# First sequence's projections by halves of the heads, and the last two ends in turn: attention with a routed feed-forward layer on one core

## The chip, the cores and the metric

One Trainium2 chip, of which the kernel uses one core. The metric is device time in microseconds (us) of one execution. PE is the matrix engine (PEld its weight loads), DVE the vector engine, ACT the scalar engine, POOL the GpSimd engine, SP the engine that here does nothing but issue DMAs (SPq and ACTq are the DMA queues that SP and ACT issue to).

## The reference

A batch x of 8 sequences of 1024 tokens, 256 wide, goes through one layer, all in float32.

```python
# attention, on layernorm(x); 16 heads of 16
q, kv = x @ Wq, x @ Wkv                       # keys and values are the same projection
q, kv = rotary(q) * SCALE, rotary(kv)
attn = softmax(einsum('bmd,bnd->bmn', q, kv)) # 1024 x 1024 per head
x = x + (einsum('bij,bjd->bid', attn, kv) @ Wout + bout)
# feed-forward, on layernorm(x), 8192 tokens, 8 experts
scores = softmax(xf @ gate_w.T)               # 8192 x 8
vals, idx = top_k(scores.T, 1024)             # each expert takes its 1024 best tokens
y = layernorm(xf[idx]) * ln_w + ln_b
out = (gelu(y @ fc1.T + b1) @ fc2.T + b2) * vals
x = x + xf.at[idx].add(out)
```

## The kernel before, in words

**Attention.** The 8 sequences (b) go one after the other. Each has four groups (g) of four heads; c = 0 and c = 1 are the two halves of the 256 columns, so the first two groups need c = 0 alone and the other two c = 1. A sequence has two halves hf of 512 tokens and T = 8 tiles t of 128 tokens. A group is 16 *steps*. Scores are needed twice: `row_max` (L425) makes four of the group's 64×128·512 products a step, and DVE takes each one's maximum over 512 keys (L440); 13 steps later (LEAD) `score_pass` (L479) makes the scores of one key tile for exp on ACT (L517), the maxima having been put in through `lay_max` (L444): maxima are transposed, copied to `mrows` (L468), written to DRAM as `top_d` (L470) and read back as rows `top` (L474). Every second step `weigh_values` (L527) multiplies exps and values. So the loop starts with 13 steps of maxima alone (s = −13 to −1), then runs maxima of one step and exps of another as *pairs*, and ends with exps alone.

**Prologue** (`prologue`, L316): for one sequence, x is normalised (statistics L185, scaled L208), transposed (L217) into `xnT`, multiplied with Wq and Wkv (L357, `ps_p`), and rotated (`rotate`, L220). Rotating takes two products with the sines (`u`, L236), one with the cosines (`pe`, L238), the sum `qk` (L239) and a copy into the value tiles `v_bufs` (L242). For b = 0 the products are on DVE and read PSUM; for later sequences ACT first copies to SBUF (L230) and all is on POOL. Then, for each c, hf and s (s = 0 queries, 1 keys), `qk` is transposed and `split_halves` (L261) makes two float32r parts `hi` and `lo`, which SP writes to DRAM (`q_d`, `k_d`, L257) twice over; `split_steps` (L289) does so with differences of neighbouring key tiles (`s_d`). `load_keys`, `load_steps` and `load_queries` (L396 to L420) read them back group by group.

**Epilogue** (`epilogue`, L602): for half a sequence, the attention output `ao` is transposed into `aoT` (L612), multiplied with Wout (L619, `ps_o`), added to the residual `xr` (L627), normalised to `xf` (L208), transposed (L661), multiplied with the gate (L667, `ps_g`), copied (`lg`, L675), transposed back (`ps_gt`, L678), put through a softmax over 8 experts (L681 to L693), transposed again (`ps_sc`), copied (`turned`, L700) and written into `by_expert` (L703); twice normalised rows go to `rows_d` in DRAM (L708).

**What sets the order.** The program is issued by hand in one order; every engine takes its instructions in that order. Prologues and epilogues are generators that stop at each `yield`. After each step `run_pieces` (L720) advances them: a piece of kind "x" is *heavy* and takes the one place that a step has while only maxima run and that every odd step has later; an integer is a wait of so many steps. `run_loads` (L758) issues loads when they are due and their data is written. Before the loop, the first prologue is advanced until the keys of c = 0 are written. After the loop `finish` runs the last sequence's two ends, first the half hf = 0, then hf = 1:

```python
        finish(urgent)
        for hf in range(2):
            if finished.pop((NG * B - 1, hf), None):
                ends.append(Task(epilogue(B - 1, hf)))
        finish(ends)
```

Tiles of a pool with one buffer per tag make the next user of the tag wait for the last: `aoT` serves `aoT` and `xfT`, `xf` the normalised rows, `lg` both `lg` and `turned`, `m` (four PSUM buffers) all of transposes, projections, maxima and weighted values.

**Selection and experts.** The 1024th best score of each expert is found by 30 rounds of bisection over `by_expert` (count L897, total over partitions L901, L904, L907); then places and token lists are made, rows gathered from `rows_d` (L1030), and the experts run (L1046 to L1084).

Of the kernel before, what the change touches and what calls it, by code (L numbers as in the profile page):

```python
# [19 lines left out]
P = 128  # L20
# [7 lines left out]
def preln_attention_moe_kernel(  # L28
# [58 lines left out]
        pattern=[[NB, E], [0, NB]], channel_multiplier=-1,  # L87
    )
    cand = [const.tile([P, 1], I32, name=f"cand{i}") for i in range(2)]

# [5 lines left out]
    with ExitStack() as actx:  # L96
# [120 lines left out]
                nc.tensor.transpose(pt[:, t * P : (t + 1) * P], src(t), ident)  # L217
            return pt

        def rotate(b, t, pp, qk):  # L220

            hd = DH // 2
            first = b == 0
            eng = nc.vector if first else nc.gpsimd
            if first:
                pe = side.tile([P, 2 * D], F32, tag="pe", name="pe")
                raw = pp
            else:
                pe = side.tile([P, 2 * D], F32, tag="pe", name="pe")
                nc.scalar.copy(pe, pp)  # L230
                raw = pe
            v4 = raw.rearrange("p (h a d) -> p h a d", a=2, d=hd)
            u = side.tile([P, 2 * H, DH], F32, tag="u", name="u")
            for a in range(2):
                s3 = sin[:, t, a, :].unsqueeze(1).to_broadcast([P, 2 * H, hd])
                eng.tensor_tensor(u[:, :, a * hd : (a + 1) * hd], v4[:, :, 1 - a, :], s3, ALU.mult)  # L236
            c4 = cos[:, t, :].unsqueeze(1).unsqueeze(1).to_broadcast([P, 2 * H, 2, hd])
            eng.tensor_tensor(pe.rearrange("p (h a d) -> p h a d", a=2, d=hd), v4, c4, ALU.mult)  # L238
            nc.gpsimd.tensor_tensor(  # L239
                qk.rearrange("p a d -> p (a d)"), pe, u.rearrange("p h d -> p (h d)"), ALU.add  # L240
            )
            kd = v_bufs[b % 2][:, t, 0 : H * VS].rearrange("p (h d) -> p h d", d=VS)[:, :, 0:DH]  # L242
            nc.gpsimd.tensor_copy(kd, qk[:, 1, :].rearrange("p (h d) -> p h d", d=DH))


        pending = []
# [14 lines left out]
        def split_halves(b, hf, c, s, pt):  # L261

            q_d, k_d, _ = halves[b]
            first = b == 0 and c == 0
            hi = side.tile([P, QW], F32R, tag="hi", name="hi")
            lo = side.tile([P, QW], F32R, tag="lo", name="lo")
            full = None
            if first:
                nc.scalar.copy(hi, pt)
                nc.vector.tensor_tensor(lo, pt, hi.bitcast(F32), ALU.subtract)  # L270
            if not first or s == 1:
                full = side.tile([P, QW], F32, tag="full", name="full")
# [12 lines left out]
            return full  # L285
# [30 lines left out]
        def prologue(b):  # L316

            q_d = dram.tile([2, D, 4, QW], F32, tag="q_d", name=f"q_d{b}", bufs=2)
            k_d = dram.tile([D, 4, N], F32, tag="k_d", name=f"k_d{b}", bufs=2)
            s_d = dram.tile([D, 4, N], F32, tag="s_d", name=f"s_d{b}", bufs=2)  # L320
            halves[b] = (q_d, k_d, s_d)
            if b == 0:
                xts = [xt_first, load_x(b, 1)]
            else:
                xts = [load_x(b, hf) for hf in range(2)]
                yield 6 if b == 1 else 2
            qks = []

            def normalised(hf):
                stats = yield from row_stats(xts[hf], "a", 2 if b == 0 else 1)  # L330
                scaled(nc.vector if b == 0 else nc.gpsimd, xts[hf], xts[hf], stats)

            yield from normalised(0)
            if b > 0:
                yield from normalised(1)
            yield 3
            for hf in range(2):
                yield "x"
                xnT = one.tile([P, DC, QW], F32, tag="T", name=f"xnT_{b}_{hf}")
                for c in range(DC):  # L340
                    pt = transposed(lambda t: xts[hf][:, t, c * P : (c + 1) * P])
                    nc.scalar.copy(xnT[:, c, :], pt)
                qk = side.tile([P, T2, 2, D], F32, tag="qk", name=f"qk_{b}_{hf}")
                qks.append(qk)
                if hf == 0:

                    yield (2 * T * NG * (b - 1) - 5,)
                other = normalised(1) if b == 0 and hf == 0 else None
                for j in range(T2):
                    if other is not None:  # L350
                        kind = next(other, None)
                        if kind is not None:
                            yield kind
                    yield "x"
                    pp = ps_m.tile([P, QW], F32, tag="m", name="ps_p")
                    for c in range(DC):
                        nc.tensor.matmul(  # L357
                            pp,
                            lhsT=xnT[:, c, j * P : (j + 1) * P],
                            rhs=wqkv[:, c].rearrange("p a d -> p (a d)"),  # L360
                            start=(c == 0),
                            stop=(c == DC - 1),
                        )
                    rotate(b, T2 * hf + j, pp, qk[:, j])
                if other is not None:
                    yield from other
            for c in range(DC):
                fulls = []
                for hf in range(2):
# [232 lines left out]
        def epilogue(b, hf):  # L602
# [3 lines left out]
            eng = nc.vector if last else nc.gpsimd  # L606
            xt = residual(b, hf)
            yield "x"
            aoT = one.tile([P, DC, QW], F32, tag="aoT", name=f"aoT_{b}_{hf}")
            for c in range(DC):  # L610
                pt = transposed(lambda t: ao[:, T2 * hf + t, c * P : (c + 1) * P])
                nc.scalar.copy(aoT[:, c, :], pt)  # L612
# [14 lines left out]
                nc.vector.tensor_tensor(sl, po, sl, ALU.add)  # L627

            stats = yield from row_stats(xt, "b")
            xf = one.tile([P, T2, D], F32, tag="xf", name=f"xf_{b}_{hf}")  # L630
# [27 lines left out]
            xfT = one.tile([P, DC, QW], F32, tag="aoT", name=f"xfT_{b}_{hf}")  # L658
# [168 lines left out]
        for hf in range(2):  # L827
            if finished.pop((NG * B - 1, hf), None):
                ends.append(Task(epilogue(B - 1, hf)))
        finish(ends)  # L830


    ctx.enter_context(tc.manual_schedule())
# [55 lines left out]
    with tc.tile_pool(name="ps_sel", bufs=2, space=PSUM) as ps_sel:  # L889
# [3 lines left out]
        now, then = cand  # L893
        nc.vector.memset(now, 1 << 29)
        for bit in range(29, -1, -1):
            cnt = it.tile([P, 1], F16, tag="cnt", name="cnt")
            nc.vector.tensor_scalar(  # L897
                ge, by_expert, now.bitcast(F32), None, ALU.is_ge, ALU.add, accum_out=cnt
            )
            tot = ps_sel.tile([P, 1], F32, tag="tot", name="tot")  # L900
            nc.tensor.matmul(tot, lhsT=same, rhs=cnt, start=True, stop=True)  # L901

            drop = it.tile([P, 1], I32, tag="drop", name="drop")
            nc.vector.tensor_scalar(  # L904
                drop, tot, float(K) - 0.5, float(1 << bit), ALU.is_lt, ALU.mult
            )
            nc.vector.scalar_tensor_tensor(  # L907
                then, drop, (1 << bit) >> 1, now, ALU.bitwise_xor, ALU.bitwise_xor
            )
            now, then = then, now  # L910
# [261 lines left out]
```

## Time and profile before

| | |
|---|---|
| runs | 2281.76, 2284.6, 2285.13 us; median 2284.6 |
| profiled execution, own time | 2283.41 us |
| its span in the trace | 2281.6 us |
| granted TensorE clock, mean | 0.962 |
| busy: PE, DVE, ACT, POOL | 2090.1 (92%), 1658.9 (73%), 1361.4 (60%), 1228.0 (54%) us |
| start, no maxima | 0 to 54.6 us |
| maxima alone | 54.6 to 94 us |
| maxima and exps in pairs | 94 to about 1660 us |
| exps alone | to about 1690 us |
| last two ends | to 1729.3 us |
| selection | to about 1790 us |
| experts | to 2281 us |

The stages are read from the timeline: the first maximum (L433) begins at 54.60, the first reduce after the first exps at 94.06, the first count (L897) at 1729.30. A matmul's end is modelled, so a busy PE may also be a slow or a waiting one. The granted clock is a share of full speed; the mean hides a stretch of 0.50 between 38 and 95 us. The execution's own time is 1.8 us more than its span.

### The profile page before, as it was taken

The page shows a single profiled execution, that of the slowest core. Times are in us where ns is not written, and L with a number is a line of the kernel's source. Part 1 is how long each engine was busy: PE and PEld are TensorE (multiplying, and loading weights), DVE is VectorE, ACT ScalarE, POOL GpSimd, SP SyncE. Part 2 cuts the span into 40 slices and gives each one's busy share as a digit, 9 for nine tenths or more (in the row PEclk, how much of TensorE's full clock was granted, in tenths as well). Part 3 has the DMA queues.
Part 4 walks back from the last instruction along what each step waited for, and adds up shares of the span by engine and source line. Part 5 has one row for each costly group of instructions (what it writes and reads, how often), then busy time and mean ns, then how long its engine had stood idle before and what let it go on. Part 6 is the DMA issues. An engine that isn't in the chain of part 4 may idle for free. (4 is left out here: it accounts for less than half of the span.)

```text
span 2281.6 us, 34611 instructions
## 1 busy us (share of the span) xinstructions
PE 2090.1 (92%) x12484; PEld 1106.4 (48%) x12484; DVE 1658.9 (73%) x3218; ACT 1361.4 (60%) x1742; POOL 1228.0 (54%) x1243
## 2 busy tenths in 40 slices
PE   4899899999999999999999999999971599999998
PEld 2444444444444444444444444444431366666665
DVE  4888888988898899889889988899926533333311
ACT  1378777877787877878777777778750011111111
POOL 4257658657584857758594765724331133333432
PEclk8699999999999999999999999999985699999999
DMA  4611633542363246236324722642113033332321
GB/s 162 244 66 67 242 113 132 204 166 88 122 236 101 85 173 238 81 121 233 118 76 171 248 76 87 219 153 86 45 43 112 20 75 75 75 72 66 78 38 27
DMA packets 154586, 275.67 MB, mean 121 GB/s; under 512 B 15152, under 2 KB 67760, under 8 KB 154288
## 3 DMA queue, kind: packets, MB, share of 16 engines
q1 hardware_dynamic: 140944, 254.80, 32.4%
q0 software_dynamic: 12288, 17.05, 4.6%
q8 instruction: 98, 1.61, 0.3%
q10 hardware_dynamic: 1184, 1.62, 0.2%
q14 instruction: 72, 0.59, 0.1%
HBM read 146.02 MB, written 127.14 MB: 120 GB/s over the span
## 5 line engine op out<-in xcount | busy, mean ns | idle before, releaser
L440 DVE TENSOR_REDUCE mx<-ps_x 128x1 f32<-128x512 f32 x2048 | 1265.1, 681 | 175.4 <-PE ps_x L433 161.5
L517 ACT ACTIVATE e<-ps_s 128x1024 f32<-128x1024 f32 x1024 | 995.8, 1025 | 102.2 <-PE ps_x L433 41.2
L433 PE MATMUL ps_x<-k,q 64*128 64x512 f32 x2048 | 727.2, 455 | 36.7 <-DMA q<-q_d 22.8
L484 PE MATMUL ps_s<-q,s 64*128 64x512 f32 x2048 | 621.8, 428 | 9.1 <-ACT e L517 5.8
L433 PEld LDWEIGHTS ps_x<-k,q 64*128 64x128 f32 x2048 | 352.0, 187 | 434.3 <-DVE mx L440 290.0
L536 PE MATMUL ps_av<-e,v 128*32 128x512 f32 x4096 | 494.0, 600 | 7.9 <-DVE mx L440 1.6
L551 POOL TENSOR_TENSOR av<-av,avp 128x512 f32<-128x512 f32 x191 | 243.3, 1274 | 411.6 <-ACT avp L549 400.7
L1066 ACT ACTIVATE hT<-ps_h,b 128x512 f32<-128x512 f32 x128 | 87.9, 687 | 431.3 <-PE ps_h L1059 431.3
L484 PEld LDWEIGHTS ps_s<-q,s 64*128 64x128 f32 x2048 | 313.7, 185 | 48.0 <-ACT e L517 30.4
L1084 POOL DMA_INDIRECT out<-o,idx x64 | 110.0, 1719 | 288.6 <-DVE o L1083 127.8
L1059 PE MATMUL ps_h<-yT,w 128*128 128x512 f32 x512 | 234.0, 604 | 0.9 <-DVE yT L1046 0.9
L1082 DVE TENSOR_TENSOR o<-ps_o,b2b 128x256 f32<-128x256 f32 x64 | 27.1, 424 | 282.2 <-PE ps_o L1074 282.2
L1074 PE MATMUL ps_o<-w,hT 128*128 128x256 f32 x1024 | 226.7, 380 | 0.0
L536 PEld LDWEIGHTS ps_av<-e,v 128*32 128x32 f32 x4096 | 107.3, 109 | 243.4 <-issue 163.8
L1074 PEld LDWEIGHTS ps_o<-w,hT 128*128 128x128 f32 x1024 | 192.8, 190 | 29.1 <-issue 4.3
L549 ACT COPY avp<-ps_av 128x512 f32<-128x512 f32 x192 | 112.6, 586 | 146.7 <-PE ps_av L536 144.1
L1059 PEld LDWEIGHTS ps_h<-yT,w 128*128 128x128 f32 x512 | 95.4, 192 | 102.0 <-issue 99.4
L357 PE MATMUL ps_p<-wqkv,xnT 128*128 128x512 f32 x256 | 127.5, 625 | 4.5 <-DVE mx L440 4.1
L1030 POOL DMA_INDIRECT g<-rows_d,idx x64 | 69.1, 1080 | 79.0 <-DVE idx L1023 59.8
L236 POOL TENSOR_TENSOR u<-pe,sin 128x256 f32<-128x256 f32 x112 | 79.2, 730 | 51.9 <-ACT pe L230 51.9
L275 POOL CAST hi<-full 128x512 fp32r<-128x512 f32 x60 | 36.7, 612 | 104.0 <-ACT full L273 73.9
L239 POOL TENSOR_TENSOR qk<-pe,u 128x512 f32<-128x512 f32 x64 | 81.7, 1277 | 15.6 <-DVE pe L238 11.2
(152 smaller groups left out, 1874.5 us busy)
## 6 DMA issues: line engine op xcount, KB each, us to landing
k<-k_d SPq DMA_DIRECT2D x64, 512.0 KB
q<-q_d SPq DMA_DIRECT2D x128, 256.0 KB
s<-s_d SPq DMA_DIRECT2D x64, 512.0 KB
q_d<-hi SPq DMA_DIRECT2D x32, 512.0 KB
q_d<-lo SPq DMA_DIRECT2D x32, 512.0 KB
k_d<-hi SPq DMA_DIRECT2D x32, 512.0 KB
k_d<-lo SPq DMA_DIRECT2D x32, 512.0 KB
s_d<-dhi SPq DMA_DIRECT2D x32, 512.0 KB
```

The source lines that it names most:

```text
L357: nc.tensor.matmul(pp, lhsT=xnT[:, c, j * P : (j + 1) * P], rhs=wqkv[:, c].rearrange("p a d -> p (a d)"), start=(c == 0), stop=(c == DC - 1),)
L433: nc.tensor.matmul(pt, lhsT=q[r : r + 64, h // 2, j * P : (j + 1) * P], rhs=k[r : r + 64, h // 2, kh * QW : (kh + 1) * QW], start=True, st ...
L440: nc.vector.tensor_reduce(grp[i]["mx"][:, kh, h, j : j + 1], pt, AX.X, ALU.max)
L484: nc.tensor.matmul(pt[:, h % 2, :], lhsT=ones_r[r : r + 64, :] if last else k[r : r + 64, pair, kt * P : (kt + 1) * P], rhs=(top_bufs[half ...
L517: nc.scalar.activation(e.rearrange("p h q -> p (h q)"), pt.rearrange("p h q -> p (h q)"), AF.Exp, scale=DH**-0.5,)
L536: nc.tensor.matmul(pa[HS * h : HS * (h + 1), :], lhsT=v_bufs[b % 2][:, kt, c : c + HS], rhs=es[h // 2][:, h % 2, :], start=(n == 0), stop= ...
L549: nc.scalar.copy(part, pa)
L551: (nc.vector if end else nc.gpsimd).tensor_tensor(av, av, part, ALU.add)
L1059: nc.tensor.matmul(ph, lhsT=weights[e][0][:, c, f * P : (f + 1) * P], rhs=yT[:, c, :], start=(c == 0), stop=(c == DC - 1),)
L1066: nc.scalar.activation(hT[:, f, :], ph, AF.Gelu_apprx_tanh, bias=b1[:, e * FC + f : e * FC + f + 1])
L1074: nc.tensor.matmul(po, lhsT=hT[:, f, j * P : (j + 1) * P], rhs=weights[e][1][:, f, :], start=(f == 0), stop=(f == FC - 1),)
L1084: nc.gpsimd.indirect_dma_start(out=out_rows[:, :], out_offset=bass.IndirectOffsetOnAxis(ap=idx[:, t : t + 1], axis=0), in_=o, in_offset=No ...
```

## The change

There are three edits.

1. *Prologue of the first sequence.* `project` and `rotate` take a column half c and a number n of halves. For b = 0 the projections of c = 0 alone (256 columns: q and k of 8 heads) are made for all eight tiles ahead of the loop; those of c = 1 are eight heavy pieces, each with its rotation, given out one to a step while the maxima run alone, and rotated by ACT and POOL as in later sequences. The second half's normalisation stands ahead of all projections, no longer between them. The second `xnT` of b = 0 takes the tag `aoT`, and the first two pairs of halves of the keys take a tile of the exps' tag `e`.
2. *Last two ends.* They are advanced in turn, one piece each. The second end (hf = 1) uses the tags `T` and `xr` where it used `aoT` and `xf`.
3. *Bisection.* The count (two tiles) and `drop` become fixed tiles, no longer tiles of the pool `it`.

```diff
+    counts = [const.tile([P, 1], F16, name=f"count{i}") for i in range(2)]
+    drop = const.tile([P, 1], I32, name="drop")
...
-        def rotate(b, t, pp, qk):
+        def rotate(b, t, pp, qk, c, n):
...
-            first = b == 0
+            first = b == 0 and c == 0
             eng = nc.vector if first else nc.gpsimd
+            W, nh = 2 * n * P, 2 * n * P // DH
+            pe = side.tile([P, 2 * D], F32, tag="pe", name="pe")[:, 0:W]
+            raw = pp
+            if not first:
                 nc.scalar.copy(pe, pp)
                 raw = pe
...
+        def project(b, t, xnT, qk, c, n):
+            pp = ps_m.tile([P, QW], F32, tag="m", name="ps_p")[:, 0 : 2 * n * P]
+            for kc in range(DC):
+                w = wqkv[:, kc, :, c * P : (c + n) * P]
+                nc.tensor.matmul(
+                    pp,
+                    lhsT=xnT[:, kc, t % T2 * P : (t % T2 + 1) * P],
+                    rhs=w.rearrange("p a d -> p (a d)") if n == DC else w,
+                    start=(kc == 0),
+                    stop=(kc == DC - 1),
+                )
+            rotate(b, t, pp, qk, c, n)
...
-            hi = side.tile([P, QW], F32R, tag="hi", name="hi")
-            lo = side.tile([P, QW], F32R, tag="lo", name="lo")
+            if first and s == 1:
+                both = prob.tile([P, 2, QW], F32R, tag="e", name="kl")
+                hi, lo = both[:, 0, :], both[:, 1, :]
+            else:
+                hi = side.tile([P, QW], F32R, tag="hi", name="hi")
+                lo = side.tile([P, QW], F32R, tag="lo", name="lo")
...
+            if b == 0:
+                xnTs = []
+                yield from normalised(0)
+                yield "x"
+                xnTs.append(turned(0))
+                yield from normalised(1)
+                for hf in range(2):
+                    if hf == 1:
+                        yield "x"
+                        xnTs.append(turned(1))
+                    for j in range(T2):
+                        yield "x"
+                        project(b, T2 * hf + j, xnTs[hf], qks[hf][:, j], 0, 1)
...
             for c in range(DC):
                 fulls = []
+                if b == 0 and c > 0:
+                    for t in range(T):
+                        yield "x"
+                        project(b, t, xnTs[t // T2], qks[t // T2][:, t % T2], c, 1)
...
-            aoT = one.tile([P, DC, QW], F32, tag="aoT", name=f"aoT_{b}_{hf}")
+            own = last and hf == 1
+            aoT = one.tile([P, DC, QW], F32, tag="T" if own else "aoT", name=f"aoT_{b}_{hf}")
...
-        finish(ends)
+        while ends:
+            for task in list(ends):
+                task.advance(n_steps)
+                if task.kind is None:
+                    ends.remove(task)
...
-            cnt = it.tile([P, 1], F16, tag="cnt", name="cnt")
+            cnt = counts[bit % 2]
...
-            drop = it.tile([P, 1], I32, tag="drop", name="drop")
```

More of the change, by code (lines that the diff above doesn't have):

```diff
@@ L218, in transposed @@
             return pt
-        def rotate(b, t, pp, qk):
+        def rotate(b, t, pp, qk, c, n):
             hd = DH // 2
-            first = b == 0
+            first = b == 0 and c == 0
             eng = nc.vector if first else nc.gpsimd
[L225 to L229, printed above, removed]
+            W, nh = 2 * n * P, 2 * n * P // DH
+            pe = side.tile([P, 2 * D], F32, tag="pe", name="pe")[:, 0:W]
+            raw = pp
+            if not first:
                 nc.scalar.copy(pe, pp)
@@ L232, in rotate @@
             v4 = raw.rearrange("p (h a d) -> p h a d", a=2, d=hd)
-            u = side.tile([P, 2 * H, DH], F32, tag="u", name="u")
+            u = side.tile([P, 2 * H, DH], F32, tag="u", name="u")[:, 0:nh, :]
             for a in range(2):
-                s3 = sin[:, t, a, :].unsqueeze(1).to_broadcast([P, 2 * H, hd])
+                s3 = sin[:, t, a, :].unsqueeze(1).to_broadcast([P, nh, hd])
                 eng.tensor_tensor(u[:, :, a * hd : (a + 1) * hd], v4[:, :, 1 - a, :], s3, ALU.mult)
-            c4 = cos[:, t, :].unsqueeze(1).unsqueeze(1).to_broadcast([P, 2 * H, 2, hd])
+            c4 = cos[:, t, :].unsqueeze(1).unsqueeze(1).to_broadcast([P, nh, 2, hd])
             eng.tensor_tensor(pe.rearrange("p (h a d) -> p h a d", a=2, d=hd), v4, c4, ALU.mult)
+            qk = qk[:, :, c * P : (c + n) * P]
             nc.gpsimd.tensor_tensor(
-                qk.rearrange("p a d -> p (a d)"), pe, u.rearrange("p h d -> p (h d)"), ALU.add
-            )
-            kd = v_bufs[b % 2][:, t, 0 : H * VS].rearrange("p (h d) -> p h d", d=VS)[:, :, 0:DH]
+                qk,
+                pe.rearrange("p (a d) -> p a d", a=2),
+                u.rearrange("p h d -> p (h d)").rearrange("p (a d) -> p a d", a=2),
+                ALU.add,
+            )
+            c0, c1 = c * P // DH * VS, (c + n) * P // DH * VS
+            kd = v_bufs[b % 2][:, t, c0:c1].rearrange("p (h d) -> p h d", d=VS)[:, :, 0:DH]
             nc.gpsimd.tensor_copy(kd, qk[:, 1, :].rearrange("p (h d) -> p h d", d=DH))
+        def project(b, t, xnT, qk, c, n):
[10 more added lines that the diff above has]
+            rotate(b, t, pp, qk, c, n)
         pending = []
@@ L331, in normalised, with turned @@
                 scaled(nc.vector if b == 0 else nc.gpsimd, xts[hf], xts[hf], stats)
[L333 to L339, printed above, removed]
+            def turned(hf):
+                tag = "aoT" if b == 0 and hf == 1 else "T"
+                xnT = one.tile([P, DC, QW], F32, tag=tag, name=f"xnT_{b}_{hf}")
                 for c in range(DC):
@@ L342, in prologue @@
                     nc.scalar.copy(xnT[:, c, :], pt)
[L343 to L353, printed above, removed]
-                    yield "x"
[L355 to L364, printed above, removed]
@@ L365, in prologue @@
-                if other is not None:
-                    yield from other
+                qks.append(side.tile([P, T2, 2, D], F32, tag="qk", name=f"qk_{b}_{hf}"))
+                return xnT
+            if b == 0:
[11 more added lines that the diff above has]
+                        project(b, T2 * hf + j, xnTs[hf], qks[hf][:, j], 0, 1)
+            else:
+                yield from normalised(0)
+                yield from normalised(1)
+                yield 3
+                for hf in range(2):
+                    yield "x"
+                    xnT = turned(hf)
+                    if hf == 0:
+                        yield (2 * T * NG * (b - 1) - 5,)
+                    for j in range(T2):
+                        yield "x"
+                        project(b, T2 * hf + j, xnT, qks[hf][:, j], 0, DC)
@@ L367, in prologue @@
             for c in range(DC):
                 fulls = []
+                if b == 0 and c > 0:
+                    for t in range(T):
+                        yield "x"
+                        project(b, t, xnTs[t // T2], qks[t // T2][:, t % T2], c, 1)
                 for hf in range(2):
@@ L629, in epilogue @@
             stats = yield from row_stats(xt, "b")
-            xf = one.tile([P, T2, D], F32, tag="xf", name=f"xf_{b}_{hf}")
+            xf = one.tile([P, T2, D], F32, tag="xr" if own else "xf", name=f"xf_{b}_{hf}")
             scaled(eng, xf, xt, stats)
@@ L657, in epilogue @@
             yield "x"
-            xfT = one.tile([P, DC, QW], F32, tag="aoT", name=f"xfT_{b}_{hf}")
+            xfT = one.tile([P, DC, QW], F32, tag="T" if own else "aoT", name=f"xfT_{b}_{hf}")
             for c in range(DC):
```

## The prediction

> **What bounds the kernel now.** I read the page first: PE 92% busy, DVE 73%, and its chain holds only the closing DMA, so it decides nothing here. The slices show where PE is not the bound: the first two and those around 1660 to 1790. The edits lie in just these places, so I read three timelines: start to first maximum, first maximum to first exp, last two ends to first count. A row gives start, duration, engine, line, operation, and in brackets the idle time before it with its releaser.
>
> The start:
>
> ```profile
> 10.23 1.38 DVE L208 TENSOR_SCALAR x<-x,mv_a,rs_a 128x256 f32<-128x256 f32 x4 [1.50 <-POOL rs_a L190]
> ...
> 34.18 0.37 SPq L257 DMA_DIRECT2D q_d<-hi  x1
> 34.63 1.26 POOL L239 TENSOR_TENSOR qk<-pe,u 128x512 f32<-128x512 f32 x1
> ...
> 54.60 6.52 PE L433 MATMUL ps_x<-k,q 64*128 64x512 f32 x12 [17.89 <-DMA q<-q_d]
> ```
>
> The first maximum waits for keys and queries that went through DRAM; their first write is issued at 34.18, just as POOL's last rotation sum begins. Between them the DMA engines are the limit. The windows (columns: stretch, length, busy time of PE, PEld, DVE, ACT, POOL, then granted clock, DMA share, GB/s) show them full to the end of the eight writes:
>
> ```profile
> 45.00:46.00 1.00, 0.00 (x0) 0.00 (x0) 0.00 (x0) 0.00 (x0) 1.00 (x3) 0.50 1.04 391
> 46.00:47.00 1.00, 0.00 (x0) 0.00 (x0) 0.00 (x0) 0.00 (x0) 0.94 (x2) 0.50 0.11 39
> ```
>
> So those 20.4 us (34.18 to 54.60) are bytes: they move as a block, and faster halves inside it gain nothing.
>
> The maxima, 54.6 to 94. DVE sets the pace (one maximum per 0.612 us, 2.45 a step of four) at a granted clock of 0.50, until a hole of over 4 us on PE and DVE:
>
> ```profile
> 81.25 0.51 SPq L257 DMA_DIRECT2D s_d<-dhi  x1
> 83.29 0.51 SPq L257 DMA_DIRECT2D s_d<-dlo  x1
> 83.90 0.56 SPq L257 DMA_DIRECT2D q_d<-hi  x1
> 85.78 0.37 SPq L257 DMA_DIRECT2D q_d<-lo  x1
> 86.24 0.49 SPq L470 DMA_DIRECT2D top_d<-mrows  x1
> 89.68 1.51 SPq L474 DMA_DIRECT2D top<-top_d  x2
> ...
> 92.81 0.80 PE L484 MATMUL ps_s<-top,ones_r 64*128 64x512 f32 x2 [4.25 <-DMA top<-top_d]
> ...
> 94.06 6.75 DVE L440 TENSOR_REDUCE mx<-ps_x 128x1 f32<-128x512 f32 x11 [4.39 <-PE ps_x L433]
> ```
>
> The maxima's rows (mrows) lie ready at 78.53 (ACT's copy, 78.28 + 0.25), but SP issues top_d only at 86.24: ahead of it in the queue stand four writes of the second half of the heads, each waiting for POOL.
>
> The last two ends run one after the other:
>
> ```profile
> 1697.06 1.38 DVE L208 TENSOR_SCALAR xf<-xr,mv_b,rs_b 128x256 f32<-128x256 f32 x4 [1.47 <-POOL rs_b L190]
> ...
> 1710.56 0.69 DVE L627 TENSOR_TENSOR xr<-ps_o,xr 128x512 f32<-128x512 f32 x1 [6.11 <-PE ps_o L619]
> ...
> 1729.30 0.74 DVE L897 TENSOR_SCALAR_CACHE_REDUCE ge<-by_expert,cand 128x512 uint8<-128x512 f32 x1 [5.26 <-DMA rows_d<-rows]
> ```
>
> ```profile
> 1725.12 0.63 SPq L708 DMA_DIRECT2D rows_d<-rows  x1
> ```
>
> No engine is full here; each end is a chain of waits, and the first count waits for the landing of rows_d, which it does not read: its count tile's memory was last that of other data.
>
> **The start, term by term.** Nothing changes up to the xnT of the first half (13.6). Then DVE takes the second half's statistics at once (before, four of them 6.50–8.72, then POOL 1.5): 11.6 to 13.75, xf at 15.25–16.63. A rotation now covers 256 of 512 columns. On DVE the full one is 2×0.416 + 0.679 = 1.51 in rows, 1.43 in spacing; half of it, with the fixed part that stays, I put at 0.9. On POOL the sum was 1.26 and the copy of v 0.40; the sum's price at 384 columns is 0.99 and at 128 0.45, so 0.73 at 256, copy 0.29, with gaps 1.05 a tile. POOL is the slowest of the three: first pe ready at 17.5, and 17.5 + 8×1.05 = 25.9 for its last sum, against 34.63 + 1.26 = 35.89. PE must keep up: four tiles by 18.25, transposes 1.7, copy 0.6, four more tiles: 23.6. The first write follows the transposes of the first queries (23.65) by 1.25 (before, 32.93 to 34.18): 24.9 for 34.18, **−9.3** (bounds −8.3 and −10.3, from POOL at 1.17 and 0.93 a tile). Own tiles for the keys' halves free four writes of a wait, but the DMA engines behind are full: nothing.
>
> PE's own price: 16 instructions 512 wide took 7.13 at full clock (0.446 each), 8 instructions 256 wide of ps_o 1.89 (0.236): 64×0.236 − 32×0.446 = 0.8 more PE time for the first sequence. The Trainium skill speaks against this edit ("Perfetto Trace Analysis", Matmuls in Optimizing Tensor Performance: "Larger matmuls are more efficient than smaller matmuls, when possible."), and these rows agree, 6% per column; by that rule alone the total would be 0.8 smaller. I count none of it here, because PE waits for POOL in the start and for DVE beside the maxima.
>
> **Beside the maxima.** Eight projections come one to a step. At half clock their four instructions take 4×0.427 (the 512 wide ones loaded weights every 0.855 from 12.8 to 16.4), the step's four maxima about as much (two instructions as wide took 0.80 at 92.81). That is 3.42 of PE against DVE's 2.45: +0.97 if the clock stays at 0.50, +7.8 in all. At full clock it needs half and hides: 0. The two bounds hang on the clock. It rose 2.7 us after PE began the dense pairs at 92.81, and 3 us into the ps_o burst (1707.0 to 1710). The projection steps leave PE no gap, so I take a step and a half at the slow rate: +1.5. Four transposes of the second half, which cost DVE gaps of 0.27 each, thin out to two before the first exp: −0.6. Together **+0.9**. POOL takes 2×0.45 + 0.73 + 0.73 + 0.29 with gaps = 2.75 a tile for these rotations, a little over the step of 2.45: 2.4 us late after eight, which the two buffers of pe and u cover; without that cover the pieces, not the maxima, slip.
>
> **The hole.** In the changed order on SP, top_d follows right behind the loads of s; the halves' writes of the second heads come later. It then goes when mrows is ready, 6.6 us before step 0's maxima are done, where the way through top_d took 86.24 to 92.81 = 6.57: the hole of 4.39 closes, **−4.4**. What is late next is the paired stage, which runs on PE (95 to 100: 4.79 of 5). The second top_d now waits behind s_d's dlo instead; it is needed eight steps (24 us) later. The second heads' last two transposes with their copies now lie among the pairs, where PE is the bound: at most eight 128-wide instructions, 1 us: **+1.0** (bounds 0, 1). Keys of group 2 are needed only at step 19.
>
> **The end.** In turn, PE transposes the second ao right after the first ps_o: ps_o of the second runs at 1694.6–1698.4 instead of 1707.0–1712.25. The first end pays: its last statistics queue on DVE behind the second's additions, stats done at 1699.65 (before 1695.58), xf 1701.15, and by the old distance (xf to ps_gt's end 4.96) ps_gt at 1706.1. The second's last statistics stand behind that on DVE: xf 1708.6, ps_gt 1713.5. Its exp queues on ACT behind the first's two by_expert issues (1.18 the second time, 2.03 the first): 1715.0; scores 1715.9; by_expert issued 1716.9–1718.1; landing 1.6 (as top's) to 3.4 (as rows_d's, 1725.75 to 1729.2): first count about 1720.8 for 1729.30, **−8.5** (bounds −5 and −9.6). Of this some 3.1 is the counts' own tiles, which no longer wait for rows_d: it landed that much behind what by_expert needs. The 30 rounds of counts keep their length.
>
> **The sum.** −9.3 + 0.9 − 4.4 + 1.0 − 8.5 = −20.3. The profiled execution's own time is 2283.41 (span 2281.6), 1.2 below the median of the runs, 2284.6. So 2283.4 − 20.3 = 2263.1, and 2264.3 as a median: 2264.
>
> **Rivals.**
> 1. The clock stays at 0.50 through all eight projections: +7.8 instead of +1.5, 6.3 later: 2270.6. For it: the windows 55 to 60 and 70 to 75 show 0.50 with PE at 4.99 and 4.97 of 5 busy. Against: those maxima wait for DVE, and a wait inside a modelled busy time is not seen. The Trainium skill ("TensorE: Matmul & The Clock Gate", Part 1) gives some 3.4 us of idleness before half clock and as much of sustained work before full clock; 2.7 and 3 us above agree with it, the 40 us at half clock do not plainly.
> 2. The ends stay serial through waits of their own (single lg tile, ACT's queue), and only the counts' tiles count: −3.1 for −8.5, 2269.7.
> 3. The front does not do what it says: the time gained at the start comes back as later waits (group 1 or 2 not ready, POOL behind), and −8.5 remains: 2276.
> 4. Slower: the half clock lives on into the pairs. Two steps there take 6.05 at full clock (groups of ps_av at 99.08, 105.12, 111.18); the same PE work with its 16 ps_av instructions at 3.84 instead of 1.92, and the pairs at half rate, needs some 7.6: +0.77 a step. After rival 1, 20.3 − 6.3 = 14.0 us of gain are left; 18 steps at half clock use them up, and 32 steps (two groups) give 24.6 − 14.0 more than before, about 2295. Against it: before, the clock rose at once with the pairs at 95.5. For it: before, that came after a hole of 4 us. The same section of the Trainium skill reports a low clock stuck for 50 us and more; no row here shows one under dense pairs, and its time would be this rival's.
>
> **How the numbers follow.** Forecast 0.60, rival 1 0.17, rival 2 0.07, rival 3 0.05, rival 4 0.08, anything else 0.03. The most favourable bounds sum to −24.9 (2259.7), the least (+7.2 beside the maxima, −5 at the end) to −9.5 (2275.1), and rival 3 stands at 2276; one to two us for the runs' own spread make it 2258 to 2277, leaving out rival 4 and the rest. About 0.2% (4.6 us) is what a measurement can tell from no change: faster 0.87, same 0.04, slower 0.09.
>
> **What would show it.** Right: first write of q_d near 25, first maximum near 45; no hole on PE before the first exp, top loaded before PE needs it; the second ps_o ahead of the first's gate; the first count released by by_expert, not rows_d, some 20 us sooner than 1729.30. Wrong: a granted clock of 0.50 beyond the first projection steps (rivals 1, 4); POOL's sums over 1.05 a tile in the start; by_expert's last issue later than 1718 less the front's gain.

## The result and the profile after

The changed kernel took 2259.04 us (median of six runs, 2258.66 to 2264.91) against 2282.55 before: a ratio of 0.9905, interval 0.989 to 0.9921. In a second set the same kernel took 2264.34 (2263.32 to 2268.07) against 2282.74: 0.9922, interval 0.991 to 0.9934. Both gains, 23.5 and 18.4 us, are clear of noise. The two medians lie 5.3 us apart. One trace of each set shows 4.3 of it, and 3.1 of these arise while the maxima run alone, which is the main finding below. The profiled execution took 2259.03 of its own time, span 2257.3, granted clock 0.968.

The start, in the timeline of the changed kernel (line numbers have moved: the sum is L241, the writes L277, maxima L466 on PE and L473 on DVE):

```profile
23.93 0.37 SPq L277 DMA_DIRECT2D q_d<-hi  x1
...
24.71 0.73 POOL L241 TENSOR_TENSOR qk<-pe,u 128x256 f32<-128x256 f32 x1
...
36.71 0.81 SPq L429 DMA_DIRECT2D k<-k_d  x2
...
42.78 6.52 PE L466 MATMUL ps_x<-k,q 64*128 64x512 f32 x12 [16.52 <-DMA q<-q_d]
```

The first write goes out 10.25 us sooner (34.18 before), the first maximum 11.82 sooner (54.60). The writes still fill the DMA engines; the windows show the same full share up to their end, now at 36:

```profile
34.00:36.00 2.00, 0.00 (x0) 0.00 (x0) 0.00 (x0) 0.00 (x0) 1.17 (x1) 0.50 0.94 354
36.00:37.00 1.00, 0.00 (x0) 0.00 (x0) 0.00 (x0) 0.00 (x0) 0.00 (x0) 0.50 0.02 8
```

The maxima, in the timelines of DVE and SP:

```profile
52.06 2.48 DVE L473 TENSOR_REDUCE mx<-ps_x 128x1 f32<-128x512 f32 x4 [1.22 <-PE ps_x L466]
55.64 9.66 DVE L473 TENSOR_REDUCE mx<-ps_x 128x1 f32<-128x512 f32 x16 [1.10 <-PE ps_x L466]
...
68.72 16.83 DVE L473 TENSOR_REDUCE mx<-ps_x 128x1 f32<-128x512 f32 x28 [0.49 <-PE ps_x L466]
```

```profile
67.09 0.33 SPq L503 DMA_DIRECT2D top_d<-mrows  x1
68.51 1.49 SPq L507 DMA_DIRECT2D top<-top_d  x2
...
75.58 0.37 SPq L277 DMA_DIRECT2D q_d<-hi  x1
```

Two projection steps cost DVE 1.22 and 1.10, then the clock is up and they cost nothing. SP issues top_d as soon as ACT has copied mrows (66.81 + 0.26), far ahead of the second heads' writes, and from 68.72 DVE runs through the first exps (78.10) without a gap: the hole of 4.39 us is gone.

The end, on DVE and on ACT:

```profile
1677.08 0.69 DVE L663 TENSOR_TENSOR xr<-ps_o,xr 128x512 f32<-128x512 f32 x1 [0.85 <-PE ps_o L655]
...
1680.24 0.69 DVE L663 TENSOR_TENSOR xr<-ps_o,xr 128x512 f32<-128x512 f32 x1 [1.39 <-PE ps_o L655]
...
1705.94 0.75 DVE L937 TENSOR_SCALAR_CACHE_REDUCE ge<-by_expert,cand 128x512 uint8<-128x512 f32 x1 [4.40 <-DMA by_expert<-turned]
```

```profile
1697.45 2.10 ACTq L739 DMA_DIRECT2D by_expert<-turned  x2
1699.59 0.23 ACT L722 ACTIVATE z<-z 128x32 f32<-128x32 f32 x1 [2.17 <-DMA by_expert<-turned]
1702.20 0.26 ACT L736 COPY turned<-ps_sc 32x128 f32<-32x128 f32 x1 [2.38 <-DMA by_expert<-turned]
```

The second end's first addition comes 3.2 us after the first end's second (17.8 before), and the first count is released by by_expert, no longer by rows_d. ACT's two rows show the new waits that the turn brings: the second end's exp behind two issues, and its copy into `turned` behind the landing of the first end's.

Four places in each trace carry all that follows: the issue of the first write of q_d, the first maximum, the second laying of maxima (DVE's reduce into `parts` for the second half of the first group, which lies behind the first exps), and the first count. From the second laying on, the traces of before and after stay 15.1 to 15.8 us apart at the layings up to 1463 us (17.3 at the last ones, 15.7 again at the second addition to xr): between these two traces nothing comes back in the paired stage.

### The profile page after: what moved, and what is told of

Same layout as the page of the kernel before. It is cut to its first block, busy times and chain, and to the rows that moved or that the text cites. A ratio compares the mean times of both kernels' runs of the same rounds, so it can differ in the third digit from the quotient of the medians.

```text
span 2257.3 us, 34734 instructions
## 1 busy us (share of the span) xinstructions
PE 2077.7 (92%) x12516; PEld 1106.2 (49%) x12516; DVE 1656.5 (73%) x3218; ACT 1364.0 (60%) x1750; POOL 1247.2 (55%) x1283
## 5 line engine op out<-in xcount | busy, mean ns | idle before, releaser
L473 DVE TENSOR_REDUCE mx<-ps_x 128x1 f32<-128x512 f32 x2048 | 1264.3, 682 | 172.5 <-PE ps_x L466 159.2
L550 ACT ACTIVATE e<-ps_s 128x1024 f32<-128x1024 f32 x1024 | 995.5, 1025 | 88.5 <-PE ps_x L466 42.8
L466 PE MATMUL ps_x<-k,q 64*128 64x512 f32 x2048 | 721.1, 451 | 35.3 <-DMA q<-q_d 21.3
L466 PEld LDWEIGHTS ps_x<-k,q 64*128 64x128 f32 x2048 | 349.0, 185 | 429.8 <-DVE mx L473 285.2
L256 PE MATMUL ps_p<-wqkv,xnT 128*128 128x512 f32 (+1 forms) x288 | 130.7, 581 | 5.8 <-DVE mx L473 4.7
L237 POOL TENSOR_TENSOR u<-pe,sin 128x256 f32<-128x256 f32 (+1 forms) x128 | 86.2, 695 | 68.5 <-ACT pe L231 68.5
L241 POOL TENSOR_TENSOR qk<-pe,u 128x512 f32<-128x512 f32 (+1 forms) x72 | 83.3, 1157 | 7.2 <-DVE pe L239 2.2
L231 ACT COPY pe<-ps_p 128x512 f32<-128x512 f32 (+1 forms) x64 | 35.9, 560 | 83.6 <-PE ps_p L256 82.3
```

What stands on the lines that cost most here:

```text
L256: nc.tensor.matmul(pp, lhsT=xnT[:, kc, t % T2 * P : (t % T2 + 1) * P], rhs=w.rearrange("p a d -> p (a d)") if n == DC else w, start=(kc == 0),
L466: nc.tensor.matmul(pt, lhsT=q[r : r + 64, h // 2, j * P : (j + 1) * P], rhs=k[r : r + 64, h // 2, kh * QW : (kh + 1) * QW], start=True, st ...
L473: nc.vector.tensor_reduce(grp[i]["mx"][:, kh, h, j : j + 1], pt, AX.X, ALU.max)
L550: nc.scalar.activation(e.rearrange("p h q -> p (h q)"), pt.rearrange("p h q -> p (h q)"), AF.Exp, scale=DH**-0.5,)
```

## Experiments

Fourteen rows, one trace each. "Load to maximum" runs from the issue of the first key load, "to laying" from the first maximum to the second laying, "end" from the second addition to xr to the first count; all in us. The ratio is that of the times to the kernel before, with its interval.

| kernel | first write | load to maximum | to laying | end | ratio |
|---|---|---|---|---|---|
| before | 34.18 | 7.81 | 46.25 | 36.54 | 1 |
| counts_only | 34.75 | 5.59 | 45.19 | 35.97 | 0.9991 (0.9982–1.0) |
| turns_only | 35.65 | 7.53 | 45.29 | 30.37 | 0.997 (0.996–0.998) |
| later_halves | 35.24 | 5.68 | 40.93 | 37.44 | 0.9971 (0.9962–0.998) |
| front_only | 23.93 | 6.33 | 49.56 | 37.25 | 0.9947 (0.9933–0.996) |
| changed | 23.93 | 6.07 | 42.80 | 28.86 | 0.9905 (0.989–0.9921) |
| after_again | 23.92 | 6.03 | 46.08 | 28.67 | 0.9922 (0.991–0.9934) |
| no_kl | 23.93 | 6.20 | 44.67 | 29.30 | 0.992 (0.99–0.994) |
| warm | 23.92 | 6.23 | 48.36 | 28.95 | 0.9935 (0.9923–0.9948) |
| warm_long | 24.13 | 6.33 | 50.26 | 29.03 | 0.9943 (0.9926–0.9961) |
| early_c1 | 24.15 | 7.81 | 41.86 | 28.97 | 0.989 (0.9875–0.9905) |
| ends_sp | 24.33 | 5.97 | 47.06 | 26.94 | 0.9893 (0.9874–0.9912) |
| best_early | 23.92 | 6.18 | 41.88 | 26.53 | 0.9888 (0.9869–0.9906) |
| best_late | 23.93 | 7.66 | 41.87 | 26.99 | 0.9894 (0.9878–0.991) |

The table leaves out the paired stage, and that stage is not the same in every trace. From the second laying to the second addition to xr, the kernel before, counts_only and turns_only took 1591.9, 1598.0 and 1599.1 us, although no edit lies there (1588.7 to 1599.1 over all fourteen). So single times differ by several us for reasons outside the change, and the readings below go by stretch. A part of it is a wait that all fourteen traces have: at the start of the second sequence, where its first maximum is due, PE stands idle for 4.6 to 5.8 us until the queries are loaded. First the kernel before, then the changed one:

```profile
253.07 0.76 PE L433 MATMUL ps_x<-k,q 64*128 64x512 f32 x1 [4.96 <-DMA q<-q_d]
```

```profile
237.58 0.76 PE L466 MATMUL ps_x<-k,q 64*128 64x512 f32 x1 [4.76 <-DMA q<-q_d]
```

Behind it the granted clock is at 0.50 for 3.4 us in the kernel before and for 6.8 us in turns_only. At the start of the third sequence PE waits 2.0 to 3.7 us for `top`. Neither the prediction nor any edit here is about these waits.

### Each part alone

**front_only**: the changed kernel with the old ends and the old counts.

```diff
-        while ends:
-            for task in list(ends):
...
+        finish(ends)
...
-            cnt = counts[bit % 2]
+            cnt = it.tile([P, 1], F16, tag="cnt", name="cnt")
```

> The changed prologue alone; the last two ends one after the other and the counts' tiles as before. If the parts of the change are independent, the second last addition of the last half's end comes 15.7 us sooner than before (the distance read between the two traces) and the way from there to the first count stays at 36.5 us: about 15.7 us faster, 14 to 17.5. If the gain of the start were partly an effect of the ends, or came back in the last stage, less than 13. From the load of the first keys to the first maximum, 6.1 us if the own tile of the keys' halves is what shortened it, anything from 6 to 8 if that is chance.

Measured: 2272.45 against 2284.73, 12 us faster and not 15.7. The start is as early as in the changed kernel and the end takes 37.25; what is missing is in between, 49.56 us to the second laying where the changed kernel took 42.80 (the paired stage of this trace was 2.8 us shorter and hides a part). The instructions there are the same. The clock is not:

```profile
50.00:55.00 5.00, 4.81 (x12) 2.42 (x10) 3.57 (x6) 0.37 (x1) 2.60 (x5) 0.50 1.06 404
55.00:60.00 5.00, 4.80 (x13) 2.32 (x12) 3.02 (x5) 0.75 (x2) 3.33 (x7) 0.50 0.46 161
65.00:70.00 5.00, 4.83 (x15) 2.19 (x13) 3.48 (x8) 0.74 (x2) 3.22 (x7) 0.50 0.00 0
75.00:80.00 5.00, 4.56 (x15) 2.35 (x13) 3.90 (x8) 0.77 (x2) 3.87 (x8) 0.62 0.65 211
```

against the changed kernel's

```profile
50.00:55.00 5.00, 4.81 (x14) 2.42 (x12) 3.33 (x6) 0.40 (x2) 2.60 (x5) 0.50 1.07 394
55.00:60.00 5.00, 4.70 (x18) 2.52 (x18) 4.36 (x8) 0.72 (x2) 4.20 (x9) 0.86 0.47 170
60.00:65.00 5.00, 4.79 (x18) 2.75 (x18) 5.00 (x9) 0.94 (x3) 4.64 (x10) 1.00 0.81 305
```

The column before the last two is the granted clock; DVE's busy time is the third. At 0.50 DVE gets 3.0 to 3.6 of 5 us, at 1.00 all 5. This is rival 1 of the prediction, in an execution of the same instructions in which the forecast had come out: 6.8 us more, where the rival was priced at 6.3.

**turns_only** and **counts_only**: the second and the third edit of the change, each alone in the kernel before.

> The start as before, the last two ends in turn on own tiles, the counts' tiles as before, so that the first count waits for rows_d. Theory: the turn gains 7.7 us less what rows_d lands behind by_expert, in the changed kernel's trace about 1.6: 6.1 us faster (5 to 7.5). Rival: without the counts' own tiles the turn is worth little because rows_d's place in SP's queue sets the end: 0 to 3 us.

> Start and ends as before; the count and drop alone are fixed tiles. The prediction's term: 3.1 us faster. From the changed kernel's trace, by_expert lands 2.3 us after its last issue, so here at about 1727.3 instead of 1729.3: 1.9 us faster. If the first count waits for something else that lands as late as rows_d, 0.

```profile
1730.50 0.75 DVE L902 TENSOR_SCALAR_CACHE_REDUCE ge<-by_expert,cand 128x512 uint8<-128x512 f32 x1 [6.10 <-DMA rows_d<-rows]
```

```profile
1732.15 0.75 DVE L899 TENSOR_SCALAR_CACHE_REDUCE ge<-by_expert,cand 128x512 uint8<-128x512 f32 x1 [4.30 <-DMA by_expert<-turned]
```

The first row is turns_only, the second counts_only. The turn shortens the end from 36.5–37.4 (three traces) to 30.4 and gives 0.3% (some 6.9 us of 2284.7); its count still waits for rows_d. The counts' tiles change the releaser as meant, but by_expert, whose last issue was over at 1728.88, let the first count begin only at 1732.15: 3.3 us later, nearly as late as rows_d had. So they are worth about 1 us, not the 3.1 of the prediction, and in time no more than the measurement can tell (interval up to 1.0). With the turn they are worth 1.5 (30.37 to 28.86).

**later_halves**: only the place of the second heads' halves, in the kernel before.

```diff
             for c in range(DC):
                 fulls = []
+                if b == 0 and c > 0:
+                    for _ in range(T):
+                        yield "x"
```

> The kernel before, with eight empty heavy pieces ahead of the halves of c = 1, so that SP has top_d ahead of their writes; projections, ends and counts as before. Theory: the hole before the first exps closes by itself, and the second maxima's rows are laid 4.2 to 5 us sooner than before (in the changed kernel the step there was 4.2): 4 to 5 us faster. Rival: the hole is not SP's queue but the length of the way through DRAM, or POOL: 0 to 1 us.

```profile
75.42 0.33 SPq L473 DMA_DIRECT2D top_d<-mrows  x1
76.83 1.49 SPq L477 DMA_DIRECT2D top<-top_d  x2
...
82.13 0.37 SPq L257 DMA_DIRECT2D q_d<-hi  x1
```

top_d goes ahead of the writes, and the second laying comes 40.93 us after the first maximum, where the three other traces with the old start took 45.19 to 46.25: 4.3 to 5.3 us, and 0.29% of the time (6.6 us, interval 4.6 to 8.7). The hole was SP's queue, and eight empty pieces close it, without any projection being split: DVE's wait there was 4.39, 3.33 and 3.44 us in those three traces and is gone here. The 4.3 to 5.3 us are not the hole alone: 1.8 of them lie ahead of the first laying (20.06 us after the first maximum for 21.8), because the four transposes that stood there come later too, where they cost a part of it again.

### The clock beside the maxima

**after_again**: the changed kernel once more. **no_kl**: without the own tiles of the keys' halves.

> The changed kernel itself once more. In its first trace the clock rose after three projection steps, and the way from the first maximum to the second laying of maxima took 42.8 us; in the prologue-only kernel, which has the same instructions there, the clock stayed at 0.50 through all eight, and it took 49.6. If that is chance from execution to execution, the runs fall into two groups about 5 to 7 us apart, near 2259 and 2265, and this trace shows one of the two ways (about 42.8 or 49.6). If it hung on something else in the two kernels, all runs stand within 2 us of 2259 and the trace shows 42.8 again.

> The changed kernel without the own tiles of the first keys' halves (they take hi and lo as before). The prediction's term: nothing, since the DMA engines are full behind the wait; from the first write to the load of the keys 12.6 to 12.8 us, as in all kernels so far, and the same time as the changed kernel within its two groups. Rival: the halves wait for landed writes, the write block grows: 1 us or more, to 13.8 or beyond.

```diff
-            if first and s == 1:
+            if False:
```

after_again took neither 42.8 nor 49.6 but 46.08: the clock rose at 65.4 instead of 56.4.

```profile
55.00:60.00 5.00, 4.63 (x13) 2.24 (x12) 3.43 (x6) 0.55 (x2) 3.66 (x8) 0.50 0.44 157
60.00:65.00 5.00, 4.83 (x12) 2.72 (x12) 3.90 (x7) 0.37 (x1) 3.88 (x8) 0.50 0.72 283
65.00:70.00 5.00, 3.95 (x15) 1.78 (x13) 4.12 (x10) 0.82 (x3) 3.94 (x9) 0.95 0.00 0
```

So the same kernel goes different ways in different executions, graded and not in two groups. What sets the moment at which the clock rises these runs do not show, nor whether the chip has a share. That trace's span is 4.3 us longer than the first; 3.1 of this is there at the second laying. In no_kl the clock rose at 52.6, fell again at 66.2, and it took 44.67. Its writes took 12.6 us from the first issue to the load of the keys, as with the own tiles (12.8): those give nothing, as the prediction said.

**warm** and **warm_long**: 14 and 19 unused matmuls on PE while it waits for the DMAs.

```diff
+        pw = ps_m.tile([P, QW], F32, tag="m", name="ps_w")
+        for _ in range(14):
+            nc.tensor.matmul(pw, lhsT=ident, rhs=wqkv[:, 0].rearrange("p a d -> p (a d)"), start=True, stop=True)
```

> The changed kernel with 14 matmuls of 128x128x512 (their result is not used) on PE ahead of the first maximum, where it waits for DMA. If the slow projection steps come from a clock lowered by that wait, and 13 us of matmuls keep it up, the clock is 1.0 at the first maximum and the steps cost nothing: 40.5 to 41.5 us from the first maximum to the second laying, runs in one group, 2 us below the changed kernel's fast runs. If the maxima alone, with PE waiting for DVE, let the clock fall again before the projections, 42.8 or 49.6 as without them, and no gain.

> As the kernel with 14 unused matmuls, now with 19, so that PE is busy until the first maximum; with 14 it stood idle for 5.8 us before it and the clock was at 0.50 again. If half the clock in the projection steps stems from the idle PE before the first maximum, the clock is now 1.0 when the maxima begin and stays so: 40.5 to 41.5 us from the first maximum to the second laying, runs in one group. If the maxima alone, whose PE waits for DVE, are not enough work to hold the clock, it falls within the first three steps, and the way takes 42 to 50 us. The matmuls may hold up the first maximum by up to 1 us.

With 14 PE stood idle for 5.8 us and the clock was back at 0.50. With 19 PE still stood idle for 1.79 us, but the clock was at full speed at the first maximum (44.33):

```profile
40.00:45.00 5.00, 3.05 (x9) 1.01 (x7) 0.16 (x1) 0.00 (x0) 0.00 (x0) 1.00 0.97 352
45.00:50.00 5.00, 4.71 (x10) 2.17 (x10) 5.00 (x9) 0.00 (x0) 0.00 (x0) 0.69 1.04 407
50.00:55.00 5.00, 4.81 (x11) 2.63 (x12) 3.78 (x7) 0.37 (x1) 1.73 (x4) 0.50 1.08 385
```

It fell at 46.9, 2.5 us after the first maximum, while PE shows 4.71 of 5 busy, and stayed at 0.50 to 88 us: 50.26, the slowest of all. So full clock at the first maximum is not held. That the maxima are not enough work, because PE waits for DVE after each one and the modelled ends hide it, fits but is not shown; the idle 1.79 us may have a share. Heating PE beforehand is no cure; the medians of both kernels lie above the changed one's, and in both the writes of the start took 13.9 us in place of 12.6 to 12.8, for a reason that these runs do not show. Both traces had a slow paired stage too (1597.4 and 1595.9 us for the changed kernel's 1591.5), so their longer times are not the clock beside the maxima alone.

**early_c1**: the eight projections moved into the stage in which the halves pass through DRAM, rotated and summed on DVE; the halves of c = 1 keep their late place by eight empty pieces.

```diff
                 if b == 0 and c > 0:
                     for t in range(T):
-                        yield "x"
                         project(b, t, xnTs[t // T2], qks[t // T2][:, t % T2], c, 1)
+                    in_loop.append(1)
+                    for t in range(T):
+                        yield "x"
...
+        while not in_loop:
+            starts[0].advance(0)
```

> The changed kernel with the eight projections of c = 1 moved into the stage in which the halves pass through DRAM (PE and DVE idle there), rotated and summed on DVE into tiles of their own; the halves of c = 1 keep about their later place. Theory: no projection beside the maxima, so neither the two slow steps nor the eight: from the first maximum to the second laying 40.9 us, as in the kernel with delayed halves (42.8 and 49.6 with projections), and runs in one group: 2 us faster than the changed kernel's fast runs, 3 to 5 than its median. Rival 4 of the prediction: without projections the half clock lives on into the pairs: 0.77 us a step, up to 24 us slower if it holds for two groups; in the delayed kernel it rose 4.7 us after the first pair.

```profile
30.00:35.00 5.00, 4.02 (x16) 2.31 (x14) 4.86 (x17) 0.00 (x0) 2.89 (x4) 1.00 1.03 381
45.00:50.00 5.00, 5.00 (x11) 2.40 (x9) 4.67 (x8) 0.00 (x0) 0.00 (x0) 0.50 1.03 377
65.00:70.00 5.00, 4.28 (x14) 2.10 (x13) 4.12 (x8) 0.84 (x2) 1.56 (x2) 0.50 0.03 9
80.00:85.00 5.00, 4.74 (x28) 2.43 (x30) 5.00 (x9) 5.00 (x7) 2.52 (x4) 0.90 0.94 363
```

PE does that work from 26 us on and DVE from 28 to 39, beside the DMAs. The clock is then at 0.50 all through the maxima, which need no more, and rises with the pairs. Three traces with this start took 41.86, 41.88 and 41.87 us to the second laying, 1.0 more than expected, where seven with projections beside the maxima took 42.8 to 50.3. The load ahead of the first maximum took 7.81, 6.18 and 7.66 us in these three and 5.97 to 6.33 in the seven; whether the moved work has a share in that is not shown. On the same chip early_c1 took 2258.10 where the changed kernel took 2264.34, and their intervals do not overlap. In none of the fourteen traces did the half clock live on into the pairs for long; in later_halves it rose 4.7 us after the first of them. Short dips do occur: in the changed kernel's trace the clock is at 0.50 from 77 to 80, with the first pairs, and in turns_only, warm_long and best_late for 3 to 4 us after the second laying. There the way to the third laying took 25.3 to 25.4 us, and 23.7 in the other eleven, so such a dip costs 1.7 us.

### The ends, and a version that has both

**ends_sp**: a tile of its own for the second `turned`, and the first end's writes of by_expert all on SP. **best_early**: this and the moved projections. **best_late**: that, and the second group's loads later.

```diff
+            if own:
+                turned = side.tile([P, QW], F32, tag="full", name="turned")[0 : T2 * E, 0:P]
+            else:
+                turned = small.tile([T2 * E, P], F32, tag="lg", name="turned", bufs=1)
...
-                (nc.scalar if last and t % 2 else nc.sync).dma_start(
+                (nc.scalar if own and t % 2 else nc.sync).dma_start(
```

> The changed kernel with two edits in its ends: the second end's turned scores get a tile of their own, and the first end's four writes of by_expert are all issued by SP, so that ACT goes straight on to the second end's exp. Theory: the end lost its last 2 us to these two waits (exp held up 2.1 us by ACT's two issues; the second copy of turned waits for the first by_expert to land): from the second addition to xr to the first count 26.5 to 27.3 us, against 28.9 and 28.7 in the two traces of the changed kernel; 1.5 to 2.3 us faster, less than the spread of its times. If the landing of the first by_expert or the issue on SP sets the pace in any case, 28.5 to 29.

> The changed kernel with the eight projections moved into the stage in which the halves pass through DRAM, and with the two edits of the ends. If both gains add: 41 to 42 us from first maximum to second laying, 26.5 to 27.3 from the second addition to the first count, about 2 us less than the kernel with the moved projections alone (0.989 of before): 0.987 to 0.989 of before. If the ends' edits give nothing, 0.989 to 0.990.

> The same, and the loads of the second group's keys and queries issued behind the first group's s instead of at once behind the first group's keys. Over nine traces the first maximum came 5.6 to 7.8 us after the first key load was issued, with the second group's 2 MB on the same DMA engines. If that traffic is what makes it long, it now takes 5 us or less (2 MB at 385 to 400 GB/s is 5.2, and not all of it is waited for), and the time falls by 1 to 2.5 us against the kernel without this edit. If not, 5.6 to 7.8 as before; and if the second group's loads then come too late, a new hole of DVE at the second group's first maxima.

```profile
1705.03 0.25 ACT L739 COPY turned<-ps_sc 32x128 f32<-32x128 f32 x1 [0.57 <-PE ps_gt L714]
1705.48 0.23 ACT L722 ACTIVATE z<-z 128x32 f32<-128x32 f32 x1 [0.20 <-DVE z L719]
1706.92 0.26 ACT L739 COPY turned<-ps_sc 32x128 f32<-32x128 f32 x1 [1.22 <-PE ps_sc L734]
```

In ends_sp the exp follows 0.45 us after the first copy (2.43 in the changed kernel) and the second copy waits for PE alone. The end took 26.94, 26.53 and 26.99 us in three traces against 28.7 to 29.3 in the six traces with only turn and counts: 2 us, as expected. In time ends_sp overlaps the changed kernel. best_early has the lowest ratio, 0.9888, but its interval overlaps that of early_c1; it beats the kernel before clearly, and against the changed kernel the gain is seen in the traces' two stretches and not in the ratios of the first set.

best_late does not bear out its reason: 7.66 us from load to first maximum, with the second group's loads out of the way. But the test is not a clean one, since in their place the weights' loads (from 39.27) and s_d's writes (from 41.27) went to the same DMA engines. Over the fourteen traces this way takes 5.6 to 7.8 without order; what decides it stays open.

## Why the prediction was right, and by which steps

The forecast was 2264 in 2258 to 2277, a gain of 20.3; the two sets gave 2259.0 and 2264.3, gains of 23.5 and 18.4. The sign and the size were right. The terms, by the traces:

- **The start, −9.3: mechanism right, size 1.7 short.** The first write came at 24.0 (mean of ten traces with the new start) against 35.0 (mean of four with the old): −10.9, beyond the bounds; in the first pair of traces −10.25, at their edge. POOL was as sized: one tile per 1.04 us (eight sums from 17.42 to 24.71), last sum over at 25.44 for 25.9. But POOL, from which the bounds were drawn, does not set the first write: it follows PE's transposes of the first queries by 1.25 us, as foretold, and these came at 22.68 and not 23.65. PE's way there was sized too long: the first four tiles were done at 17.83 for 18.25, and the transposes with their copy took 1.3 us for 2.3. One error hid a part of it: the sum leaves 3.05 us for tiles 4 to 7, where the prediction's own price of 0.236 an instruction gives 3.8; they took 3.69. The other 1.57 of that pair's 11.82 is the way from there, above all the load, 6.07 for 7.81, which the prediction took as a fixed block of bytes; it varies with no edit (5.6 and 5.7 in two kernels with the old start).
- **Beside the maxima, +0.9: right in the profiled execution, wrong as a typical value.** There, up to the first laying, the two slow steps cost 2.3 and the transposes that no longer stand there gave back 1.6: +0.7 (22.55 us from the first maximum for 21.83). A slow step cost 1.1 to 1.2, a little over the 0.97 foretold. But the step "the projection steps leave PE no gap, so I take a step and a half" was too sure: in seven traces with these pieces the clock rose anywhere from the first step or two to after the last. Against 41.87 without projections the stage lost 0.9 to 8.4 us. The bounds 0 and +7.8 were right but for 0.6; within them it is a draw, and rival 1 deserved far more than 0.17.
- **The hole, −4.4: right in mechanism and size.** DVE's wait of 4.39 us is gone after; later_halves shows that SP's queue made it. In two other traces with the old start it was 3.3 and 3.4, so 4.4 is the upper end.
- **Two transposes in the paired stage, +1.0: not seen.** The two traces are 15.27 apart at the second laying and 15.27 at the third and fourth, with one of the two transposes behind the second laying (87.54) and the other just ahead of it (81.51). The lower bound, 0, was the right one.
- **The ends, −8.5: total nearly right, split wrong.** The traces give 37.1 (mean of three with the old ends and counts) to 29.0 (mean of six): −8.1. The turn gives 6.7 of it for 5.4, the counts' tiles 1.4 for 3.1, since the first count, released by by_expert, comes 2.1 to 3.3 us after the end of its last issue. The chain up to the second scores was met within 0.2 us (23.2 after the second addition, 23.1 foretold); then `turned` cost 1.3 more. ACT's two issues, 2.10, were in the forecast; that the copy waits for the landing of the first end's by_expert, until 1702.20, was not.
- **Rivals 2, 3 and 4** did not happen: the ends do interleave, though one wait for the single `lg` tile is there; the time gained at the start is still there at the second addition; and no trace looked at keeps half a clock among the pairs for more than 7 us at a time.

Where the clock rises early, as in the profiled execution, the misses add up to 2.7 us more gain than the forecast's 20.3 (start 2.5 and transposes 1.0 better, ends 0.8 worse); the first counts lie 23.4 apart. Where it rises late the start's surplus pays for the slow steps. So that the second set's 2264.3 meets the forecast is in part luck: two misses of opposite sign.

The Trainium skill ("TensorE: Matmul & The Clock Gate", Part 1) says that the time to full clock is one busy window of some 3.4 us, and that, the window being free-running, it varies from run to run. Its second half agrees in kind with 42.8 to 50.3 us for the same instructions; of the first, the pairs' 2.7 and 4.7 us agree in size, but under projections and maxima 10 to 41 us passed at 0.50 with PE shown 4.6 to 4.8 of 5 busy. The same part tells of short waits of PE between groups that make the clock swing. That fits no_kl, where it rose at 52.6 and fell at 66.2; these runs show the swing, not its cause.

## What to carry to other kernels

When PE work is placed beside a stage that another engine paces, price it at both clocks, and treat the clock as a draw, also where the profile shows PE busy for 4.8 of 5 us: here the price was anything from 1 to 8 us. Better is a stage where PE and DVE are truly idle, here the wait for DRAM, where the same projections left the writes' 12.6 us as they were. And look at queues for what stands ahead of a short, urgent transfer: in time eight empty pieces gave as much as the turn of the ends. Before counting a gain of a few us from one trace, look how much the stages that the edit does not touch differ from trace to trace, here up to 10 us.

## What the runs showed of the hardware

- Full clock at the first maximum does not last: after 19 matmuls and 1.79 us of idleness it held to 46.9 us, 2.5 us into the maxima, and fell to 0.50 with PE shown busy 94% from 45 to 50.
- The half clock can come back for 3 to 4 us among dense pairs (turns_only, warm_long, best_late); one such dip cost 1.7 us.
- DVE can slow when POOL works beside it: in early_c1 the same 128x256 sum from SBUF took 1.28 us while POOL made dlo (28.55 to 29.81), and 0.43 while POOL waited (33.30 to 34.15). Of its eight instances three fell beside POOL's sums and differences of two tiles (1.28, 0.79, 0.91 us); the other five took 0.42 to 0.43, one of them while POOL copied v.

```profile
28.81 1.28 DVE L246 TENSOR_TENSOR qk<-pe,us 128x256 f32<-128x256 f32 x1
...
33.60 0.43 DVE L246 TENSOR_TENSOR qk<-pe,us 128x256 f32<-128x256 f32 x1
```

- From the end of by_expert's last issue to the first count that waits for it, 2.1 (ends_sp) to 3.3 us (counts_only) passed.
